# A selective-scan and attention kernel: state sums folded in pairs on POOL, B one step further ahead, and a new spacing of the work around the scan

## The chip, the cores and the metric

The kernel runs on one core of a Trainium2 chip. The metric is device time in microseconds of one execution. The kernel before takes 1438.1 us, the median of three runs (1437.43 to 1439.29). A core has a matmul engine (PE, with a weight-load port PEld), a vector engine (DVE), a scalar engine (ACT), a general engine (POOL) and a queue that issues transfers (SP). Each works through its own list of instructions in order, and waits on semaphores where it needs another's result. Matmuls write to eight banks of PSUM; everything else lives in SBUF.

## The reference

Input x is 4 images of 64x64 pixels with 96 channels. Two layers follow each other; layer normalisation and casts are left out here.

```python
# layer 0: group norm over 32 groups, layer norm, then a selective scan over the 4096 pixels
proj = xn @ W_in + b_in                      # value u, gate g, delta d, and A, B, C of 96 channels x 16 states
h = d * (A * h) + d * (B * u)                # a recurrence over the pixels, per channel and state
y = sigmoid(g) * sum_over_states(C * h)
x = x + (y @ W_out + b_out)
# layer 1: linear attention (no softmax), then an FFN with fp8 products and fp16 sums
t = t + attention(ln(t)) ; t = t + ffn(ln(t))
```

The scan is most of the work: 96 x 16 = 1536 recurrences over 4096 pixels for each of 4 images.

## The kernel before, in words

An image (a batch b) is cut into 8 chunks of 512 pixels, and a chunk into 12 tiles: 4 state groups (sh) of 4 states, times 3 channel groups (cg) of 32 channels. A tile is 128 recurrences (32 channels x 4 states on the partitions) over 512 pixels. There are 384 tiles, and one tile is one step of the main loop. For each tile:

- PE projects A, B and C (three matmuls each, line 175, a high and low split of float32) into the PSUM banks "A" (two), "B" (one) and "C" (one).
- ACT copies B with its bias to SBUF (b_copy, line 595, tile bu), and POOL multiplies it by du, the delta times the value (b_mul, line 598).
- DVE multiplies A by d in place in PSUM (a_mul, line 607), scans (line 614, tile h), and multiplies C by h (c_mul, line 632, tile ch). ACT keeps the scan's last column for the next chunk (keep, line 624).
- After every third tile PE sums the four states of a state group: three matmuls with the matrix fold, one for each channel group on its own 32 columns of the array (state_sum, line 645), added up over the four groups in the bank "Y". As the profile counts them, each is two instructions.

The order of work is written out by hand. The main loop (line 870) goes through steps s from FRONT = -22 on, and in each records: a_proj(s+1), c_proj(s), keep of the last tile, b_mul(s+1), scan(s), a_mul(s+1), c_mul(s); then whatever was registered for this step with at(step, fn), in the order of registration; then b_proj(s+2) and b_copy(s+2). ffn and tail are themselves called at their first step, and register their pieces then, so these stand last in a step. Nothing reorders the lists later. The pieces registered around the scan:

- front (line 496), for the chunk that comes about two later: the group norm is applied (POOL, lines 504 and 507), layer norm (stats on DVE, rstd on POOL, lines 327 and 328, apply on ACT, line 354), transposed, split into high and low (DVE lo, three transfers on SP), and projected to d, du and gate. d and du are each copied by 12 transfers on SP to tiles of 128 partitions (copies, line 531), tiles d4 and du4 with five buffers for three per chunk.
- tail (line 654): gating (yg), output projection, residual, layer norm, and the Gram matrix of the attention; attn_matrix (line 701) turns the latter into one 97x96 matrix per batch.
- ffn (line 740), for the batch before: attention, residual, layer norm, transpose, three hidden matmuls with relu and fp8 rounding (relu, quant), output projection, rounding and bias (y16, yb), store (o). It runs FFN0 = 15 steps into the next batch, one FFN per chunk; for the last batch it runs after the last tile (drain = True), an FFN every DRAIN_EVERY = 2 steps.
- group_norm (line 476), for the next batch: x is loaded, transposed by PE into the one bank "B" (gx_ps), and ACT takes sum and sum of squares from there (sums, line 412), eight times, from step GN0 = 22 of the batch on every GN_EVERY = 6 steps, loads 8 steps ahead; before them first() takes the mean of the first piece. Its last pieces give the scale and shift that front applies (diagonal builds the tile gdg, spread multiplies it out).

The small matmuls of front, tail, ffn and group norm share the two banks "M". Lengths in steps are given as places in a chunk of 12: "step 13" of a chunk is step 1 of the next.

Of the kernel before, what the change touches and what calls it, by code (L numbers as in the profile page):

```python
# [8 lines left out]
F32 = mybir.dt.float32  # L9
# [7 lines left out]
P = 128  # L17
# [20 lines left out]
FRONT = -22  # L38
GN0, GN_EVERY = 22, 6
FFN0 = 15  # L40
XBUFS = 2 * NCH + 5
DRAIN_EVERY = 2
# [3 lines left out]
def conv_attn_hybrid_kernel(  # L46
# [56 lines left out]
    nc.scalar.dma_start(bet, ln_beta.unsqueeze(1))  # L103
    raw0 = big.tile([C, A0], F32, tag="x", name="raw0", bufs=XBUFS)
    nc.scalar.dma_start(raw0, w_in[:, 0:A0])
    raws, brows = {}, {}
    for k, c0 in enumerate((B0, A0, C0)):
        for cg in range(NCG):
            t = big.tile([C, 32 * S], F32, tag="xat", name=f"raw{k}{cg}", bufs=NCH + 2)
            n0 = c0 + cg * 32 * S  # L110
            nc.scalar.dma_start(t, w_in[:, n0 : n0 + 32 * S])
            raws[k, cg] = t
        brows[k] = work.tile([NCG, 32 * S], F32, tag="ch", name=f"brow{k}", bufs=6)
        nc.scalar.dma_start(
            brows[k], b_in[c0 : c0 + C * S].rearrange("(g n) -> g n", g=NCG)
        )
# [108 lines left out]
    def bias(k):  # L225
        ps = bank("Y", [4, NSH * P], f"bias_ps{k}")
        for cg in range(NCG):
            for n, t in enumerate((betd[0], betd[0], betd[1])):
                nc.tensor.matmul(
                    ps, lhsT=t[:, cg, :], rhs=w_bac[k][:, n, cg],  # L230
                    start=(cg == 0 and n == 0), stop=(cg == NCG - 1 and n == 2),
                )
        row = work.tile([NCG, NSH * P], F32, tag="ch", name=f"bias{k}", bufs=6)
        nc.vector.tensor_tensor(
            row.rearrange("g (s c) -> g s c", s=S),
            ps[0:NCG].rearrange("g (s c) -> g s c", s=S),
            brows[k].rearrange("g (c s) -> g s c", s=S), ALU.add,
        )
        t_ps = bank("C", [P, NSH, NCG], f"biast_ps{k}")
        for sh in range(NSH):  # L240
            nc.tensor.transpose(
                t_ps[:, sh, :], row[:, sh * P : (sh + 1) * P], ident[:NCG, :NCG]
            )
        nc.vector.tensor_copy(b_bac[:, k], t_ps.rearrange("p h g -> p g h"))
# [17 lines left out]
    b2_q = const.tile([P, C], F32, name="b2_q")  # L262
    w1_sb = big.tile([P, NK, C], F32, tag="x", name="w1_sb", bufs=XBUFS)
    nc.scalar.dma_start(w1_sb, w1.rearrange("(m p) k -> p m k", p=P))
    w2_sb = big.tile([C, HID], F32, tag="x", name="w2_sb", bufs=XBUFS)
    nc.scalar.dma_start(w2_sb, w2)
    b1_sb = big.tile([NK, P], F32, tag="x", name="b1_sb", bufs=XBUFS)
    nc.scalar.dma_start(b1_sb, b1.rearrange("(m p) -> m p", p=P))
    b2_sb = big.tile([P, C], F32, tag="x", name="b2_sb", bufs=XBUFS)
    nc.scalar.dma_start(b2_sb, b2.partition_broadcast(P))  # L270
# [106 lines left out]
    class GroupNorm:  # L377
# [67 lines left out]
        def diagonal(self):  # L445
            self.dg = small.tile([C, 2, C], F32, tag="gdg", name=f"gdg_{self.b}", bufs=1)
            for k in range(2):
                nc.scalar.activation(
                    self.dg[:, k, :], ident[0:C, 0:C], AF.Copy, scale=self.m[:, k : k + 1]
                )  # L450
# [25 lines left out]
    def group_norm(b, s0):  # L476
        q = {}

        def make():
            q["g"] = GroupNorm(b)  # L480
            q["g"].first()

        def call(name, *args):
            getattr(q["g"], name)(*args)

        at(s0 + GN0 - 6, make)
        for n in range(NCH):
            at(s0 + GN0 + GN_EVERY * n - 8, load_x, b, n)
            at(s0 + GN0 + GN_EVERY * n, call, "sums", n)
        e = s0 + GN0 + GN_EVERY * (NCH - 1) + 1  # L490
        for n, name in enumerate(("moments", "mean", "root", "diagonal", "spread")):
            at(e + n, call, name)
# [79 lines left out]
    class Tile:  # L572
# [20 lines left out]
        def b_copy(self):  # L593
            self.bu = work.tile([P, TC], F32, tag="bu", name=f"bu_{self.nm}", bufs=4)
            nc.scalar.activation(self.bu, self.b_ps, AF.Identity, bias=self.bias(0))  # L595
# [16 lines left out]
        def scan(self):  # L612
            self.h = work.tile([P, TC], F32, tag="h", name=f"h_{self.nm}", bufs=3)
            nc.vector.tensor_tensor_scan(  # L614
                self.h, self.a_ps, self.bu,
                0.0 if self.i == 0 else state[self.sh, self.cg], ALU.mult, ALU.add,
            )
# [12 lines left out]
        def c_mul(self):  # L630
            self.ch = work.tile([P, TC], F32, tag="ch", name=f"ch_{self.nm}", bufs=6)
            nc.vector.scalar_tensor_tensor(  # L632
                self.ch, self.c_ps, self.bias(2), self.h, ALU.add, ALU.mult
            )

    tiles = {}
    y_ps = {}

    def state_sum(b, i, sh):

        g = b * NCH + i
        if sh == 0:
            y_ps[g] = bank("Y", [C, TC], f"y_ps_{b}_{i}")
        for cg in range(NCG):
            nc.tensor.matmul(  # L645
                y_ps[g][cg * 32 : (cg + 1) * 32, :], lhsT=fold,
                rhs=tiles.pop(g * NT + NCG * sh + cg).ch,
                start=(sh == 0), stop=(sh == NSH - 1),
                tile_position=(0, 32 * cg), skip_group_check=True,
            )  # L650
# [3 lines left out]
    def tail(b, i, s0):  # L654
# [39 lines left out]
        at(s0 + 6, lambda: ln.apply(xa, t))  # L694
        at(s0 + 7, gram)
        at(s0 + 8, keep)

# [3 lines left out]
    def attn_matrix(b, s0):  # L701
# [35 lines left out]
        for n, fn in enumerate((gram_out, gk, kv, ff, r)):  # L737
            at(s0 + 8 + n, fn)

    def ffn(b, i, s0, drain):  # L740
# [19 lines left out]
        def transpose():  # L760
            ps = bank("B" if drain else "M", [C, TC], f"xq_ps_{nm}")
            for j in range(J):
                nc.tensor.transpose(ps[:, j * P : (j + 1) * P], v["xn"][:, j, :], ident)
            v["xq"] = work.tile([C, TC], F8, tag="xq", name=f"xq_{nm}")
            nc.scalar.activation(v["xq"], ps, AF.Copy, saturate=False)

        def hidden(m):
            v["h", m] = bank(("C", "Y", "M")[m] if drain else "M", [P, TC], f"h_ps{m}_{nm}")
            nc.tensor.matmul(
# [3 lines left out]
        def relu(m):  # L773
            if m == 0:
                v["hq"] = work.tile([P, NK, TC], F8, tag="hq", name=f"hq_{nm}", bufs=1)
            h16 = work.tile([P, TC], F16, tag="h16", name=f"h16_{m}_{nm}")
            nc.scalar.copy(h16, v["h", m])  # L777
            hr = work.tile([P, TC], F16, tag="hr", name=f"hr_{m}_{nm}")
            bias = b1_q[:, m : m + 1]
# [9 lines left out]
        def project_out():  # L789
            ps = v["ps"] = bank("M", [P, J, C], f"y2_ps_{nm}")  # L790
            for j in range(J):
# [6 lines left out]
        def round_out():  # L798
            v["y16"] = work.tile([P, J, C], F16, tag="y16", name=f"y16_{nm}", bufs=1)
            nc.scalar.copy(v["y16"], v["ps"])  # L800

        def bias_out():
            v["yb"] = work.tile([P, J, C], F16, tag="yb", name=f"yb_{nm}", bufs=1)
            nc.gpsimd.tensor_tensor(  # L804
# [3 lines left out]
        def store():  # L808
            o = work.tile([P, J, C], F32, tag="o", name=f"o_{nm}", bufs=1)
            nc.gpsimd.tensor_tensor(o, t, v["yb"], ALU.add)  # L810
# [6 lines left out]
        at(s0 + 4, apply)  # L817
        at(s0 + 5, transpose)
        for m in range(NK):
            at(s0 + 6 + m, hidden, m)  # L820
            at(s0 + 7 + m, relu, m)
            at(s0 + 7 + m + drain, quant, m)
        at(s0 + 10 + drain, project_out)
        at(s0 + 11 + drain, round_out)
        at(s0 + 12 + drain, bias_out)
        at(s0 + 13 + drain, store)


# [15 lines left out]
    for b in range(B):  # L844
        for i in range(NCH):
            s0 = (b * NCH + i) * NT
            front(b, i, s0)
            for sh in range(NSH):
                at(s0 + NCG * (sh + 1), state_sum, b, i, sh)
            at(s0 + NT, tail, b, i, s0 + NT)  # L850
            if b < B - 1:
                at(s0 + NCH * NT + FFN0, ffn, b, i, s0 + NCH * NT + FFN0, False)
            else:
                e = K + FFN0 + DRAIN_EVERY * i
                at(e, ffn, b, i, e, True)
# [12 lines left out]

    s = FRONT
    while s < K or any(q >= s for q in steps):  # L870
        for k in (s, s + 1, s + 2):
            if 0 <= k < K and k not in tiles:
                tiles[k] = Tile(k)
# [4 lines left out]
        if 0 < s <= K:  # L878
            last.keep()
        if 0 <= s + 1 < K:  # L880
            tiles[s + 1].b_mul()
        if 0 <= s < K:
# [6 lines left out]
        call(s)  # L889
        if 0 <= s + 2 < K:  # L890
            tiles[s + 2].b_proj()
            tiles[s + 2].b_copy()
        s += 1
# [32 lines left out]
```

## Time and profile before

| What | Value |
|---|---|
| Median of three runs | 1438.1 us |
| The profiled execution | 1436.83 us |
| Its span, first to last instruction | 1435.1 us |
| Busy: PE, DVE, POOL, ACT | 1300.3, 1212.5, 747.2, 723.1 us |
| Granted PE clock, mean | 0.951 |
| First scan, last scan (start) | 71.1 us, 1347.5 us |
| State sums (line 645) | 768 instructions, 136.5 us busy |
| b_mul (line 598) | 384 instructions, 1286 ns each |

The profile is of one execution. "Busy" is the time in which an engine had an instruction in work; a matmul that is held up in the pipeline counts as busy. A line of the groups or of the timeline names the engine, the source line, the tiles (out<-in), the shape, and in brackets the idle time just before it and what ended it. The three parts of the span are the start (71 us: weights, first chunk's front), the loop, and what lies after the last tile (88 us).

### The profile page before, as it was taken

To read this page: it belongs to the slowest core of one execution; us is meant where nothing else is said; L and a number is where in the kernel's file an instruction comes from. 1 tells how busy PE (TensorE), PEld (TensorE's weight loads), DVE (VectorE), ACT (ScalarE), POOL (GpSimd) and SP (SyncE) were. 2 spreads that over 40 slices of the span, in tenths; PEclk is the share of its full clock that TensorE was granted. 3 is DMA by queue.
4 is the path that set the end of the run, shared out by engine and by line. 5 is a ranking of instruction groups with operands and counts; after the bars stand their busy time and mean duration, and the time that the engine had idled before them with its cause. 6 is when DMAs were issued, how large, how long until landed. Compare 5 with 4: busy or idle time off the path is not lost. (4 is left out here: it accounts for less than half of the span.)

```text
span 1435.1 us, 20740 instructions
## 1 busy us (share of the span) xinstructions
PE 1300.3 (91%) x6396; PEld 891.0 (62%) x6396; DVE 1212.5 (84%) x2309; ACT 723.1 (50%) x1658; POOL 747.2 (52%) x743
## 2 busy tenths in 40 slices
PE   2699988899999899899999998989999999999885
PEld 2356665666666666666666666666666666666562
DVE  2398988899998898899998888889999999999742
ACT  3234343433336555555555455665554555655555
POOL 3254544455554555555555555555556566545424
PEclk6699999999999999999999999999999999999955
DMA  6422222222222222222222122222222222222001
GB/s 156 107 61 56 49 55 61 48 54 54 54 59 51 69 51 56 57 47 60 60 50 70 45 62 57 58 52 58 59 49 49 51 60 59 50 49 51 12 6 44
DMA packets 81357, 80.98 MB, mean 56 GB/s; under 512 B 49617, under 2 KB 50101, under 8 KB 81246
## 3 DMA queue, kind: packets, MB, share of 16 engines
q1 hardware_dynamic: 78544, 77.22, 22.6%
q10 hardware_dynamic: 2702, 2.43, 0.7%
q8 instruction: 51, 0.84, 0.3%
q14 instruction: 60, 0.49, 0.1%
HBM read 8.72 MB, written 6.29 MB: 10 GB/s over the span
## 5 line engine op out<-in xcount | busy, mean ns | idle before, releaser
L598 POOL TENSOR_TENSOR bu<-bu,du 128x512 f32<-128x512 f32 x384 | 493.9, 1286 | 575.2 <-ACT bu L595 351.2
L614 DVE TENSOR_TENSOR_SCAN h<-Aps,state,bu 128x512 f32<-128x512 f32 x336 | 428.1, 1274 | 46.6 <-POOL bu L598 45.4
L595 ACT ACTIVATE bu<-Bps,b_bac 128x512 f32<-128x512 f32 x384 | 261.8, 682 | 398.2 <-PE Bps L175 386.2
L607 DVE SCALAR_TENSOR_TENSOR Aps<-Aps,b_bac,d 128x512 f32<-128x512 f32 x384 | 284.3, 740 | 64.5 <-PE Aps L175 63.8
L175 PE MATMUL Bps<-xs,w 128*128 128x512 f32 x768 | 271.0, 434 | 52.7 <-ACT gx_ps L412 37.6
L632 DVE SCALAR_TENSOR_TENSOR ch<-Cps,b_bac,h 128x512 f32<-128x512 f32 x384 | 285.5, 744 | 1.5 <-PE Cps L175 1.3
L175 PE MATMUL Cps<-xs,w 128*128 128x512 f32 x768 | 245.0, 401 | 3.0 <-DVE ch L632 2.9
L175 PE MATMUL Aps<-xs,w 128*128 128x512 f32 x768 | 241.7, 396 | 2.4 <-DVE h L614 2.1
L175 PEld LDWEIGHTS Bps<-xs,w 128*128 128x128 f32 x768 | 127.4, 191 | 102.1 <-ACT gx_ps L412 44.8
L175 PEld LDWEIGHTS Cps<-xs,w 128*128 128x128 f32 x768 | 142.1, 190 | 46.4 <-DVE ch L632 17.9
L175 PEld LDWEIGHTS Aps<-xs,w 128*128 128x128 f32 x768 | 145.4, 190 | 38.0 <-DVE h L614 4.1
L175 PE MATMUL Bps<-xl,w 128*128 128x512 f32 x384 | 152.6, 397 | 0.0
L175 PE MATMUL Aps<-xl,w 128*128 128x512 f32 x384 | 151.9, 395 | 0.0
L175 PE MATMUL Cps<-xl,w 128*128 128x512 f32 x384 | 151.6, 395 | 0.0
L645 PE MATMUL y_ps<-ch,fold 128*32 128x512 f32 x768 | 136.5, 605 | 0.0
L354 ACT ACTIVATE xa<-x,nmr_a,rstd_a 128x96 f32<-128x96 f32 x128 | 49.4, 457 | 105.0 <-DVE nmr_a L350 105.0
L354 ACT ACTIVATE z<-z,nmr_c,rstd_c 128x96 f32<-128x96 f32 x128 | 49.4, 457 | 78.1 <-DVE nmr_c L350 78.1
L175 PEld LDWEIGHTS Aps<-xl,w 128*128 128x128 f32 x384 | 72.8, 190 | 16.9
L175 PEld LDWEIGHTS Bps<-xl,w 128*128 128x128 f32 x384 | 72.6, 189 | 16.9
L175 PEld LDWEIGHTS Cps<-xl,w 128*128 128x128 f32 x384 | 72.8, 189 | 16.5
L787 ACT ACTIVATE hq<-hr 128x512 fp8e5<-128x512 f16 x96 | 60.6, 631 | 17.9 <-PE y_ps L793 8.2
L614 DVE TENSOR_TENSOR_SCAN h<-Aps,bu 128x512 f32<-128x512 f32 x48 | 58.1, 1211 | 11.0 <-POOL bu L598 10.9
(163 smaller groups left out, 1594.3 us busy)
## 6 DMA issues: line engine op xcount, KB each, us to landing
d<-d SPq DMA_DIRECT2D x384, 64.0 KB, 2.0
du<-du SPq DMA_DIRECT2D x384, 64.0 KB, 2.0
xl<-lo SPq DMA_DIRECT2D x64, 128.0 KB, 2.3
x<-in_x_dram SPq DMA_DIRECT2D x32, 192.0 KB, 2.8
out_dram<-o SPq DMA_DIRECT2D x32, 192.0 KB, 2.2
w<-w SPq DMA_DIRECT2D x6, 384.0 KB
xs<-lo SPq DMA_DIRECT2D x32, 64.0 KB, 2.0
raw<-in_L_conv_W_in_dram ACTq DMA_DIRECT2D x9, 192.0 KB, 4.5
```

Source lines behind the costliest of these rows:

```text
L175: nc.tensor.matmul(ps, lhsT=wt[:, n], rhs=mv, start=(n == 0), stop=(n == 2))
L354: nc.scalar.activation(dst[:, j, 0:C], src[:, j, :], AF.Identity, bias=nmr[:, j : j + 1], scale=self.r[:, j : j + 1],)
L595: nc.scalar.activation(self.bu, self.b_ps, AF.Identity, bias=self.bias(0))
L598: nc.gpsimd.tensor_tensor(self.bu, self.bu, rep["du4", self.b, self.i, self.cg], ALU.mult)
L607: nc.vector.scalar_tensor_tensor(self.a_ps, self.a_ps, self.bias(1), rep["d4", self.b, self.i, self.cg], ALU.add, ALU.mult,)
L614: nc.vector.tensor_tensor_scan(self.h, self.a_ps, self.bu, 0.0 if self.i == 0 else state[self.sh, self.cg], ALU.mult, ALU.add,)
L632: nc.vector.scalar_tensor_tensor(self.ch, self.c_ps, self.bias(2), self.h, ALU.add, ALU.mult)
L645: nc.tensor.matmul(y_ps[g][cg * 32 : (cg + 1) * 32, :], lhsT=fold, rhs=tiles.pop(g * NT + NCG * sh + cg).ch, start=(sh == 0), stop=(sh == ...
L787: nc.scalar.activation(v["hq"][:, m, :], v["hr", m], AF.Copy, saturate=False)
```

## The change

- After c_mul of an odd state group, POOL adds its ch tile to the ch tile of the even group before it (pair_sum); state_sum then runs for two groups at once, twice per chunk instead of four times.
- Tiles are made one step earlier: b_mul is recorded two steps ahead of its scan (was one), b_proj and b_copy three (were two). bu gets five buffers (four), ch eight (six), h two (three).
- tail starts one step later and its gram two; ffn starts at FFN0 = 26 and its pieces stand further apart; group norm at GN0 = 24, with its loads three steps ahead of its sums instead of eight.
- For the drain, FFN pieces use the banks C, B, Y, C and A instead of B, C, Y, M and M, and hq, y16, yb and o take the buffers of ch, d4, du4 and z. relu and quant of one piece now stand in the same step, and h16 and hr have one buffer instead of two.
- Some tiles move to other pools: raw0, w1_sb, w2_sb, b1_sb, b2_sb, and gdg, which shares a buffer with o. x has 22 buffers instead of 21.

```diff
-GN0, GN_EVERY = 22, 6
-FFN0 = 15
-XBUFS = 2 * NCH + 5
+GN0, GN_EVERY = 24, 6
+FFN0 = 26
+XBUFS = 2 * NCH + 6
...
-            self.dg = small.tile([C, 2, C], F32, tag="gdg", name=f"gdg_{self.b}", bufs=1)
+            self.dg = work.tile([C, 2, C], F32, tag="o", name=f"gdg_{self.b}", bufs=1)
...
-        at(s0 + GN0 - 6, make)
+        at(s0 + GN0 - 1, make)
         for n in range(NCH):
-            at(s0 + GN0 + GN_EVERY * n - 8, load_x, b, n)
+            at(s0 + GN0 + GN_EVERY * n - 3, load_x, b, n)
             at(s0 + GN0 + GN_EVERY * n, call, "sums", n)
...
-            self.bu = work.tile([P, TC], F32, tag="bu", name=f"bu_{self.nm}", bufs=4)
+            self.bu = work.tile([P, TC], F32, tag="bu", name=f"bu_{self.nm}", bufs=5)
...
-            self.h = work.tile([P, TC], F32, tag="h", name=f"h_{self.nm}", bufs=3)
+            self.h = work.tile([P, TC], F32, tag="h", name=f"h_{self.nm}", bufs=2)
...
+    def pair_sum(k):
+
+        t = tiles.pop(k).ch
+        s = tiles[k - NCG].ch
+        nc.gpsimd.tensor_tensor(s, s, t, ALU.add)
...
-                start=(sh == 0), stop=(sh == NSH - 1),
+                start=(sh == 0), stop=(sh == NSH - 2),
...
-        at(s0 + 7, gram)
-        at(s0 + 8, keep)
+        at(s0 + 8, gram)
+        at(s0 + 9, keep)
...
-            at(s0 + 8 + n, fn)
+            at(s0 + 10 + n, fn)
...
-                v["hq"] = work.tile([P, NK, TC], F8, tag="hq", name=f"hq_{nm}", bufs=1)
-            h16 = work.tile([P, TC], F16, tag="h16", name=f"h16_{m}_{nm}")
+                tag, bufs = ("ch", 8) if drain else ("hq", 1)
+                v["hq"] = work.tile([P, NK, TC], F8, tag=tag, name=f"hq_{nm}", bufs=bufs)
+            h16 = work.tile([P, TC], F16, tag="h16", name=f"h16_{m}_{nm}", bufs=1)
...
-            hr = work.tile([P, TC], F16, tag="hr", name=f"hr_{m}_{nm}")
+            hr = work.tile([P, TC], F16, tag="hr", name=f"hr_{m}_{nm}", bufs=1)
...
-        at(s0 + 5, transpose)
-        for m in range(NK):
-            at(s0 + 6 + m, hidden, m)
-            at(s0 + 7 + m, relu, m)
-            at(s0 + 7 + m + drain, quant, m)
-        at(s0 + 10 + drain, project_out)
-        at(s0 + 11 + drain, round_out)
-        at(s0 + 12 + drain, bias_out)
-        at(s0 + 13 + drain, store)
+        at(s0 + 6, transpose)
+        for m, d in enumerate((8, 9, 11)):
+            at(s0 + d, hidden, m)
+            at(s0 + d + 1, relu, m)
+            at(s0 + d + 1, quant, m)
+        at(s0 + (14 if drain else 17), project_out)
+        at(s0 + (15 if drain else 18), round_out)
+        at(s0 + (16 if drain else 19), bias_out)
+        at(s0 + (17 if drain else 20), store)
...
-            for sh in range(NSH):
-                at(s0 + NCG * (sh + 1), state_sum, b, i, sh)
-            at(s0 + NT, tail, b, i, s0 + NT)
+            for sh in range(0, NSH, 2):
+                for cg in range(NCG):
+                    at(s0 + NCG * (sh + 1) + cg + 1, pair_sum, s0 + NCG * (sh + 1) + cg)
+                at(s0 + NCG * (sh + 2) + 1, state_sum, b, i, sh)
+            at(s0 + NT, tail, b, i, s0 + NT + 1)
...
-                e = K + FFN0 + DRAIN_EVERY * i
+                e = K + 16 + DRAIN_EVERY * i
...
-        if 0 <= s + 1 < K:
-            tiles[s + 1].b_mul()
+        if 0 <= s + 2 < K:
+            tiles[s + 2].b_mul()
...
-        if 0 <= s + 2 < K:
-            tiles[s + 2].b_proj()
-            tiles[s + 2].b_copy()
+        if 0 <= s + 3 < K:
+            tiles[s + 3].b_proj()
+            tiles[s + 3].b_copy()
```

More of the change, by code (lines that the diff above doesn't have):

```diff
@@ L103, in conv_attn_hybrid_kernel @@
     nc.scalar.dma_start(bet, ln_beta.unsqueeze(1))
-    raw0 = big.tile([C, A0], F32, tag="x", name="raw0", bufs=XBUFS)
+    raw0 = big.tile([C, A0], F32, tag="xat", name="raw0", bufs=NCH + 2)
     nc.scalar.dma_start(raw0, w_in[:, 0:A0])
@@ L112, in conv_attn_hybrid_kernel @@
             raws[k, cg] = t
-        brows[k] = work.tile([NCG, 32 * S], F32, tag="ch", name=f"brow{k}", bufs=6)
+        brows[k] = work.tile([NCG, 32 * S], F32, tag="ch", name=f"brow{k}", bufs=8)
         nc.scalar.dma_start(
@@ L232, in bias @@
                 )
-        row = work.tile([NCG, NSH * P], F32, tag="ch", name=f"bias{k}", bufs=6)
+        row = work.tile([NCG, NSH * P], F32, tag="ch", name=f"bias{k}", bufs=8)
         nc.vector.tensor_tensor(
@@ L262, in conv_attn_hybrid_kernel @@
     b2_q = const.tile([P, C], F32, name="b2_q")
-    w1_sb = big.tile([P, NK, C], F32, tag="x", name="w1_sb", bufs=XBUFS)
+    w1_sb = work.tile([P, NK, C], F32, tag="ch", name="w1_sb", bufs=8)
     nc.scalar.dma_start(w1_sb, w1.rearrange("(m p) k -> p m k", p=P))
-    w2_sb = big.tile([C, HID], F32, tag="x", name="w2_sb", bufs=XBUFS)
+    w2_sb = work.tile([C, HID], F32, tag="ch", name="w2_sb", bufs=8)
     nc.scalar.dma_start(w2_sb, w2)
-    b1_sb = big.tile([NK, P], F32, tag="x", name="b1_sb", bufs=XBUFS)
+    b1_sb = work.tile([NK, P], F32, tag="h", name="b1_sb", bufs=2)
     nc.scalar.dma_start(b1_sb, b1.rearrange("(m p) -> m p", p=P))
-    b2_sb = big.tile([P, C], F32, tag="x", name="b2_sb", bufs=XBUFS)
+    b2_sb = work.tile([P, C], F32, tag="h", name="b2_sb", bufs=2)
     nc.scalar.dma_start(b2_sb, b2.partition_broadcast(P))
@@ L630, in c_mul @@
         def c_mul(self):
-            self.ch = work.tile([P, TC], F32, tag="ch", name=f"ch_{self.nm}", bufs=6)
+            self.ch = work.tile([P, TC], F32, tag="ch", name=f"ch_{self.nm}", bufs=8)
             nc.vector.scalar_tensor_tensor(
@@ L760, in transpose @@
         def transpose():
-            ps = bank("B" if drain else "M", [C, TC], f"xq_ps_{nm}")
+            ps = bank("C" if drain else "M", [C, TC], f"xq_ps_{nm}")
             for j in range(J):
                 nc.tensor.transpose(ps[:, j * P : (j + 1) * P], v["xn"][:, j, :], ident)
-            v["xq"] = work.tile([C, TC], F8, tag="xq", name=f"xq_{nm}")
+            tag, bufs = ("bu", 5) if drain else ("xq", 1)
+            v["xq"] = work.tile([C, TC], F8, tag=tag, name=f"xq_{nm}", bufs=bufs)
             nc.scalar.activation(v["xq"], ps, AF.Copy, saturate=False)
         def hidden(m):
-            v["h", m] = bank(("C", "Y", "M")[m] if drain else "M", [P, TC], f"h_ps{m}_{nm}")
+            v["h", m] = bank("BYC"[m] if drain else "M", [P, TC], f"h_ps{m}_{nm}")
             nc.tensor.matmul(
@@ L789, in project_out @@
         def project_out():
-            ps = v["ps"] = bank("M", [P, J, C], f"y2_ps_{nm}")
+            ps = v["ps"] = bank("A" if drain else "M", [P, J, C], f"y2_ps_{nm}")
             for j in range(J):
@@ L798, in round_out @@
         def round_out():
-            v["y16"] = work.tile([P, J, C], F16, tag="y16", name=f"y16_{nm}", bufs=1)
+            tag, bufs = ("d4", 5) if drain else ("y16", 1)
+            v["y16"] = work.tile([P, J, C], F16, tag=tag, name=f"y16_{nm}", bufs=bufs)
             nc.scalar.copy(v["y16"], v["ps"])
         def bias_out():
-            v["yb"] = work.tile([P, J, C], F16, tag="yb", name=f"yb_{nm}", bufs=1)
+            tag, bufs = ("du4", 5) if drain else ("yb", 1)
+            v["yb"] = work.tile([P, J, C], F16, tag=tag, name=f"yb_{nm}", bufs=bufs)
             nc.gpsimd.tensor_tensor(
@@ L808, in store @@
         def store():
-            o = work.tile([P, J, C], F32, tag="o", name=f"o_{nm}", bufs=1)
+            if drain:
+                o = big.tile([P, J, C], F32, tag="z", name=f"o_{nm}")
+            else:
+                o = work.tile([P, J, C], F32, tag="o", name=f"o_{nm}", bufs=1)
             nc.gpsimd.tensor_tensor(o, t, v["yb"], ALU.add)
@@ L869, in conv_attn_hybrid_kernel @@
     s = FRONT
+    made = set()
     while s < K or any(q >= s for q in steps):
-        for k in (s, s + 1, s + 2):
-            if 0 <= k < K and k not in tiles:
+        for k in (s, s + 1, s + 2, s + 3):
+            if 0 <= k < K and k not in made:
+                made.add(k)
                 tiles[k] = Tile(k)
```

## The prediction

> **What bounds the kernel now.** I read the page first, then the windows, then the waits and the timeline of one chunk. Two windows (columns: us from the start; length; busy time of PE, weight load, DVE, ACT, POOL; granted clock; DMA):
>
> ```profile
> 480.00:520.00 40.00, 36.16 (x191) 25.06 (x190) 35.12 (x65) 23.45 (x56) 21.36 (x21) 1.00 0.26 63
> 1200.00:1240.00 40.00, 39.44 (x198) 26.84 (x196) 37.16 (x70) 22.74 (x54) 23.06 (x23) 1.00 0.22 53
> ```
>
> The loop has two regimes. Where the next batch's group norm runs (480), PE idles a tenth; elsewhere (1200) PE shows full and DVE is close behind. Lengths of chunks of 12 steps come from the starts of the scans (timeline):
>
> ```profile
> 309.40 1.27 DVE L614 TENSOR_TENSOR_SCAN h<-Aps,state,bu 128x512 f32<-128x512 f32 x1
> 345.48 1.28 DVE L614 TENSOR_TENSOR_SCAN h<-Aps,state,bu 128x512 f32<-128x512 f32 x1
> 544.48 1.28 DVE L614 TENSOR_TENSOR_SCAN h<-Aps,state,bu 128x512 f32<-128x512 f32 x1 [0.68 <-POOL bu L598]
> 587.00 1.28 DVE L614 TENSOR_TENSOR_SCAN h<-Aps,state,bu 128x512 f32<-128x512 f32 x1 [0.68 <-POOL bu L598]
> 1196.52 1.28 DVE L614 TENSOR_TENSOR_SCAN h<-Aps,state,bu 128x512 f32<-128x512 f32 x1
> 1235.64 1.28 DVE L614 TENSOR_TENSOR_SCAN h<-Aps,state,bu 128x512 f32<-128x512 f32 x1
> ```
>
> So 36.1 us with neither FFN nor group norm, 42.5 with both, 39.1 with FFN alone; with group norm alone the scans give 39.9 to 41.6.
>
> "PE full" is partly back-pressure. From start to next start, a projection takes 0.70 us, a state sum 0.99; 36 projections, four sums and the small matmuls (dug 3x0.70, o_ps 0.82, a_ps 0.92, xat and gram 1.03, y2 0.51, the rest 1.5) make 36 of the 39.1. DVE's own floor: 2.50 us from scan to scan without other work, 12 times, and 6.0 of other work (stats 3x0.93, lo 0.66, du 0.65, yg 0.59, residuals 0.90, the rest 0.4): 36.0. The 3 us between are waits like these:
>
> ```profile
> 1226.86 1.28 DVE L614 TENSOR_TENSOR_SCAN h<-Aps,state,bu 128x512 f32<-128x512 f32 x1 [0.96 <-POOL bu L598]
> 1233.09 1.28 DVE L614 TENSOR_TENSOR_SCAN h<-Aps,state,bu 128x512 f32<-128x512 f32 x1 [0.96 <-POOL bu L598]
> 1210.36 0.76 DVE L607 SCALAR_TENSOR_TENSOR Aps<-Aps,b_bac,d 128x512 f32<-128x512 f32 x1 [0.49 <-PE Aps L175]
> ```
>
> Twice per chunk the scan waits for bu: ACT copies it late, behind a layer norm. In group norm PE also waits for the one B bank, where ACT takes its sums:
>
> ```profile
> 561.69 0.72 PE L175 MATMUL Bps<-xs,w 128*128 128x512 f32 x2 [1.64 <-ACT gx_ps L412]
> ```
>
> A third queue matters, SP's. The third d copy of a chunk overwrites what a_mul of tile 9 reads, so it and the 12 du copies behind it wait for that a_mul (waits of SP's own queue, and the timeline, where tile 9's a_mul ended at 1225.25):
>
> ```profile
> SPq L531 <- DVE Aps L607: 176.3, 31, 8.1
> 1225.28 2.41 SPq L531 DMA_DIRECT2D d<-d  x4
> 1227.73 7.55 SPq L531 DMA_DIRECT2D du<-du  x12
> ```
>
> **What the Trainium skill says.** "SBUF — State Buffer", "SBUF: two separate sides": VectorE and GpSimd lock each other out only where VectorE's operation has two SBUF inputs or a two-port mode. Scan, a_mul and c_mul each have one input in PSUM; the trace agrees: c_mul takes 0.745 us wholly under POOL work and 0.741 without. I charge POOL's new work nothing on DVE. "GPSIMD Engine Reference", "Elementwise — side-by-side cycle accounting": about 2.6 cycles per element for two inputs; 512 at 1.2 GHz are 1.1 us plus dispatch (an estimate); b_mul measures 1.286 and, back to back, 1.25, which I use for the add. "DMA: Bandwidth & Descriptors", "Anatomy of one DMA": a semaphore wait happens on the issuing sequencer; the SP lines above show it: everything behind waits too.
>
> **The change part by part.** Steps are counted from a chunk's first tile, so tile 12 is the next chunk's first.
>
> *Half the state sums go.* Two sums of 0.99 us per chunk, 64 in all: 63 us of PE work. PE's floor falls to 34, below DVE's 36.0; alone this is worth at most the distance to DVE.
>
> *B a step ahead.* b_copy and b_mul have one step (2.5 us) more before their scan: the two waits of 0.96 go. Their cover is the extra bu buffer. h with two buffers makes scan(s+2) wait for ACT's keep(s), behind b_copy(s+3). At step 7, where ACT waits for nmr, keep ends 2.31 us after the next scan's start and is needed at 2.50 (by 1219.69 to 1222.0): 0 us, with 0.2 to spare.
>
> *192 adds on POOL*, 1.25 us each: 7.5 per chunk, to 31 of 39. What matters is where they stand. At steps 4 to 6 POOL is clear by the time PE wants the sum (step 7): 0. At steps 10 to 13 its queue reads b_mul(12), add(9), o, b_mul(13), add(10), b_mul(14), add(11), and PE's sum at step 13 waits for add(11), with b_proj(16) and a_proj(15) behind it, and DVE's a_mul(15) behind these. b_mul(12) is now a step earlier and meets the du copies: the first tile's last one landed at 1231.71, 6.46 us after tile 9's a_mul ended. This makes a cycle, a_mul(9) to a_mul(21): a_mul 0.73; du landed 6.46 and 0.05; POOL 6x1.25 + 0.92 = 8.4, and 0.15 for semaphores; the last column group's two passes about 0.85 (between 0.33, a third of the sum, and 1.05, as after the loop), hidden 0.24, b_proj 0.70, a_proj with its latency 0.90; then DVE's six steps 15.0 and their other work 5.2. Sum 38.7, against 39.1 before. Without FFN (no o 0.92, no hidden 0.24, DVE 1.47 less): 36.1, as before. So the gain in PE work is almost wholly returned at step 13.
>
> *Group norm moved.* Its sums fall on steps 6 and 12 instead of 4 and 10. At 6, PE has slack (three short projections) and ACT does them ahead of the layer norm: about 0. At 12, x is loaded three steps ahead instead of eight, behind the du copies: 10.03 us from tile 9's a_mul to the end of their issue, 2.75 until x lands. Cycle: 0.73 + 10.03 + 2.8 + gx 0.4 + ACT and latencies 1.7 + b_proj 0.70 + a_proj 0.90, then seven DVE steps 17.5, their other work 5.85 and 0.3 = 40.9 with FFN, 39.4 without. The wait at step 13 is inside it. first() at step 23 meets the same x: from it and the next sum 3.9 more per batch (5.7 and 2.1, less what overlaps).
>
> Chunks 1 to 5 of a batch with group norm, before from the scans: 203.9, 211.8, 214.0. After: 36.1 + 4x39.4 + 3.9 = 197.6; 36.1 + 4x40.9 + 3.9 = 203.6 (FFN starts 11 steps later, so chunk 1 has none); 38.7 + 4x40.9 + 3.9 = 206.2. Together -22.3. The eleven other FFN chunks: -0.4 each, -4.4.
>
> *Buffers.* gdg now shares o's buffer: twice POOL's o stands behind the matmul that spreads gdg, a step late: 2.5 each, +5. M banks stay one use per step: 0. x's 22nd buffer: 0.
>
> *After the loop.* The last add 1.3; FFN's layer norm now ahead of the tail's in ACT's queue 2.4; against it no y2 in front of the first attention (3.0) but one attention more (1.0): +1.7. In the drain before, hq had one buffer:
>
> ```profile
> 1394.84 0.63 ACT L787 ACTIVATE hq<-hr 128x512 fp8e5<-128x512 f16 x1 [2.44 <-PE y_ps L793]
> ```
>
> Periods were 6.9 and later 5.6 us per FFN. After, hq is free but h16 and hr have one buffer each: ACT does three times copy, wait for DVE, quantise (1.52 from start to start at 1407.93), and 1.0: 5.5. Eight of these save some 5, and one non-drain FFN more lies there (8.4 us of ACT, partly in the fill): 0, between -8 and +8.
>
> *Small waits* that the two cycles leave out (a_mul(16) and (17) get their bank with 0.1 to 0.2 to spare): 0.2 x 27 chunks = +5.
>
> Sum: -22.3 - 4.4 + 5 + 1.7 + 0 + 5 = -15. The profiled execution took 1436.8 us (span 1435.1), 1.3 below the median 1438.1: 1436.8 - 15 + 1.3 = 1423, say 1424.
>
> **Rivals.**
> *The adds arrive in time* (0.2). If POOL gets through earlier than I reckon, chunks without group norm fall to DVE's floor, 36.6 with its small waits; 14 chunks gain some 2 more, chunk 1 too: 1393. For it: POOL is idle a fifth of the time; against: the du landing.
> *The cycle through POOL and SP is longer* (0.3), the slower side. Place: the sum at step 13. Each 0.1 us costs 2.7 us over 27 chunks; from 0.55 us more the gain is gone. For it: du copies for tile 14 land 11.5 us after a_mul(9) and POOL wants them at 12.4, so one us of delay in SP or POOL goes through. At 1.2 us more: 1456.
> *Nothing in sum* (0.1): the cycle 0.55 longer, 1438.
> Mine: 0.4, own range 1408 to 1433.
>
> **How the numbers follow.** A measurement of this kernel tells 0.2% (2.9 us) from no change. Faster is mine and the first rival, 0.6; same 0.1; slower 0.3. The range leaves out the tails of the two outer cases: 1390 to 1454.
>
> **What would show it.** State sums 384 instead of 768 instructions, 68 us of busy time. POOL near 990 us. Scans waiting for bu: gone but for the first tiles of a chunk. PE's state sum waiting 2 to 3 us for POOL's ch every 12 steps, at the second sum only; gx_ps waiting for DMA x at every second sum. Chunks of 38.7 and 41. I am wrong if the sum at step 13 doesn't wait (then 1393), or if it waits over 3.5 us.

## The result and the profile after

The changed kernel takes 1460.0 us (median of 4 runs, 1457.75 to 1460.16), the kernel before 1438.4 (1437.43 to 1439.29): a ratio of 1.0147, 95% interval 1.0129 to 1.0164. The change makes it slower. The prediction was 1424, range 1390 to 1454; the sign was wrong and the range too low.

The profiled execution took 1457.75 us, its span is 1456.0, 20.9 longer than before. First the same two windows (columns: us from the start; length; busy time of PE, weight load, DVE, ACT, POOL; granted clock; DMA):

```profile
480.00:520.00 40.00, 34.19 (x158) 24.04 (x157) 34.36 (x65) 21.58 (x53) 26.16 (x24) 0.96 0.21 50
1200.00:1240.00 40.00, 36.92 (x183) 26.44 (x182) 37.40 (x72) 21.91 (x52) 30.53 (x29) 1.00 0.23 54
```

At 1200, where FFN runs alone, PE is 2.5 us less busy than before, as half the state sums are gone, and POOL 7.5 more; DVE is as busy as it was. At 480, beside the group norm, PE and DVE are both less busy, PE in part because of the halved sums. The starts of the scans give the chunks (timeline of DVE; the first three lines bound two chunks with FFN and group norm, the last two one chunk with FFN alone):

```profile
551.66 1.28 DVE L614 TENSOR_TENSOR_SCAN h<-Aps,state,bu 128x512 f32<-128x512 f32 x1
...
596.14 1.27 DVE L614 TENSOR_TENSOR_SCAN h<-Aps,state,bu 128x512 f32<-128x512 f32 x1
...
642.41 1.27 DVE L614 TENSOR_TENSOR_SCAN h<-Aps,state,bu 128x512 f32<-128x512 f32 x1
...
1173.49 1.27 DVE L614 TENSOR_TENSOR_SCAN h<-Aps,state,bu 128x512 f32<-128x512 f32 x1
...
1212.22 1.27 DVE L614 TENSOR_TENSOR_SCAN h<-Aps,state,bu 128x512 f32<-128x512 f32 x1
```

With both, 44.5 and 46.3 us against 42.5 before; with FFN alone 38.7, and its neighbours 39.7 to 40.0, against 39.1. Added up over the span, from the same starts:

| part of the span | before, us | after, us | difference | predicted |
|---|---|---|---|---|
| up to the first scan | 71.1 | 70.7 | -0.4 | - |
| chunk 0 of batch 0 | 34.4 | 32.0 | -2.4 | - |
| chunks 1 to 5 of batches 0, 1, 2 (group norm) | 629.7 | 646.1 | +16.4 | -22.3 |
| chunks 6, 7 of batch 0 and 0 of batch 1 | 108.3 | 110.7 | +2.4 | 0 |
| the twelve full chunks with FFN alone | 469.4 | 469.7 | +0.3 | -4.4 |
| last chunk to its last scan | 34.7 | 35.2 | +0.5 | - |
| after the last scan | 87.6 | 91.6 | +4.0 | +1.7 |

The prediction's +5 of small waits, 0.2 us in each of 27 chunks, stands outside this column: 3 of it belong to the fifteen chunks with group norm, 2.4 to the twelve with FFN alone. So does its +5 for the buffer of gdg.

The loss is for the most part in the group norm, and there the waits name it (waits of all engines: us in total, times, longest):

```profile
DVE Aps L607 <- PE Aps L175: 120.7, 95, 7.1
...
PE gx_ps L387 <- DMA x<-in_x_dram: 38.8, 18, 4.3
...
PEld y_ps L651 <- POOL ch L643: 28.4, 23, 2.5
...
POOL bu L598 <- DMA du<-du: 22.2, 12, 3.7
```

PE waits 38.8 us for x; before, 5.7. After the first scan it is 29.4 us in twelve waits, and none before. DVE's waits for A's projection rise from 63.8 to 120.7 us. One such place step by step (timeline, the passage from chunk 4 to chunk 5 of batch 1, the longest of the nine of its kind; the a_mul of tile 9 ended at 586.76):

```profile
586.79 2.41 SPq L531 DMA_DIRECT2D d<-d  x4
...
589.24 8.34 SPq L531 DMA_DIRECT2D du<-du  x12
...
597.63 0.58 SPq L93 DMA_DIRECT2D x<-in_x_dram  x1
...
600.79 1.06 PE L387 MATMUL gx_ps<-ident,x 128*96 128x128 f32 x4 [2.61 <-DMA x<-in_x_dram]
...
603.49 1.22 PE L175 MATMUL Bps<-xs,w 128*128 128x512 f32 x2 [1.64 <-ACT gx_ps L412]
...
606.45 0.76 DVE L607 SCALAR_TENSOR_TENSOR Aps<-Aps,b_bac,d 128x512 f32<-128x512 f32 x1 [6.55 <-PE Aps L175]
```

The order is that of the prediction: third d copy, twelve du copies, then x, gx, ACT's sums, B, A, a_mul. But B's first passes take 1.22 us where they took 0.73 at 593.09, and A's 1.05 instead of 0.62. The granted clock (the last column but two) is half there, as windows around it show:

```profile
593.00:600.60 7.60, 5.08 (x23) 3.80 (x23) 6.70 (x8) 3.87 (x10) 7.28 (x7) 1.00 0.50 121
600.60:607.40 6.80, 4.97 (x13) 3.45 (x13) 0.76 (x1) 4.52 (x10) 2.37 (x2) 0.50 0.01 2
607.50:614.30 6.80, 6.80 (x39) 5.09 (x38) 6.50 (x9) 3.37 (x7) 3.05 (x3) 1.00 0.33 77
```

At the end of PE's wait for x the clock goes to half and stays there 6.8 us, so the chain behind x runs slower. Between first and last scan the trace shows eleven such stretches, 58 us in all, ten of them in group norm chunks; before there were four of 3.4 us. The Trainium skill, "TensorE: Matmul & The Clock Gate", Part 1, says that this clock is at half after an idle window of about 3.4 us and full again after a busy one. The trace agrees in the size of the stretches, 3.41 and 6.83 us. It does not agree that the window must be idle: the wait was 2.61 us, and in the 3.41 us before the clock fell PE was busy for 0.98. The last section comes back to this.

The wait at step 13 is there too (timeline, a chunk with FFN alone):

```profile
1255.93 1.05 PE L651 MATMUL y_ps<-ch,fold 128*32 128x512 f32 x4
1256.01 1.26 POOL L643 TENSOR_TENSOR ch<-ch,ch 128x512 f32<-128x512 f32 x1
...
1257.33 1.05 PE L651 MATMUL y_ps<-ch,fold 128*32 128x512 f32 x2 [0.35 <-POOL ch L643]
...
1260.12 0.76 DVE L607 SCALAR_TENSOR_TENSOR Aps<-Aps,b_bac,d 128x512 f32<-128x512 f32 x1 [1.32 <-PE Aps L175]
```

PE does two thirds of the sum, stands for add(11), and then spends a full 1.05 us on the last column group. a_mul(15) waits 1.32 us for what is queued behind.

### The profile page after: what moved, and what is told of

The parts are those of the page before. It is cut to its first block, busy times and chain, and to the rows that moved or that the text cites. A ratio compares the mean times of both kernels' runs of the same rounds, so it can differ in the third digit from the quotient of the medians.

```text
span 1456.0 us, 20065 instructions
## 1 busy us (share of the span) xinstructions
PE 1247.2 (86%) x6012; PEld 894.7 (61%) x6012; DVE 1229.5 (84%) x2309; ACT 724.2 (50%) x1658; POOL 982.7 (67%) x935
## 4 chain that ended last, share of the span: by engine, by line
PE 42%; DVE 16%; ACT 10%; SPq 9%; issue 8%; DMA 8%; POOL 7%; ACTq 0%; POOLq 0%; DVEq 0%
PE Bps L175 11%; PE Cps L175 9%; PE Aps L175 9%; SPq L531 9%; DVE h L614 4%; DVE ch L632 4%; POOL bu L598 3%; PE y_ps L651 3%; DMA du<-du 2%; ACT gx_ps L412 2%; DMA x<-in_x_dram 2%; PE dug_ps L175 2%; ACT xa L354 2%; DMA d<-d 2%; ACT z L354 2%
## 5 line engine op out<-in xcount | busy, mean ns | idle before, releaser
L607 DVE SCALAR_TENSOR_TENSOR Aps<-Aps,b_bac,d 128x512 f32<-128x512 f32 x384 | 283.9, 739 | 123.1 <-PE Aps L175 120.7
L175 PE MATMUL Bps<-xs,w 128*128 128x512 f32 x768 | 276.0, 441 | 88.0 <-ACT bu L595 46.6
L175 PE MATMUL Cps<-xs,w 128*128 128x512 f32 x768 | 249.0, 406 | 7.2 <-DVE ch L632 6.5
L643 POOL TENSOR_TENSOR ch<-ch,ch 128x512 f32<-128x512 f32 x192 | 247.1, 1287 | 0.5 <-DVE ch L632 0.5
L651 PE MATMUL y_ps<-ch,fold 128*32 128x512 f32 x384 | 88.7, 619 | 11.6 <-POOL ch L643 11.6
L354 ACT ACTIVATE xn<-x,nmr_f,rstd_f 128x96 f32<-128x96 f32 x96 | 37.0, 456 | 65.9 <-DVE nmr_f L350 65.9
```

The lines of the kernel that those rows point to most:

```text
L175: nc.tensor.matmul(ps, lhsT=wt[:, n], rhs=mv, start=(n == 0), stop=(n == 2))
L354: nc.scalar.activation(dst[:, j, 0:C], src[:, j, :], AF.Identity, bias=nmr[:, j : j + 1], scale=self.r[:, j : j + 1],)
L607: nc.vector.scalar_tensor_tensor(self.a_ps, self.a_ps, self.bias(1), rep["d4", self.b, self.i, self.cg], ALU.add, ALU.mult,)
L643: nc.gpsimd.tensor_tensor(s, s, t, ALU.add)
L651: nc.tensor.matmul(y_ps[g][cg * 32 : (cg + 1) * 32, :], lhsT=fold, rhs=tiles.pop(g * NT + NCG * sh + cg).ch, start=(sh == 0), stop=(sh == ...
```

## The experiments

Theory X: the loss is the late load of x. It is loaded three steps ahead, and SP reaches it only behind the third d copy and the du copies, which wait for the a_mul of tile 9. Theory B, the rival, lays the loss on other parts of the change, so that moving the loads does little. A further question was what each part is worth once X is out of the way: the adds, B's step, the group norm's steps.

| run | edit | median, us | ratio to before, 95% |
|---|---|---|---|
| after | the change | 1460.0 | 1.0147 (1.0129-1.0164) |
| e1 | after, loads eight steps ahead | 1404.5 | 0.9747 (0.9724-0.9770) |
| e2 | before, seven of eight loads three ahead | 1515.6 | 1.0521 (1.0497-1.0545) |
| e3 | after without adds, four sums | 1453.4 | 1.0090 (1.0072-1.0108) |
| e7 | after, du copies ahead of the third d copy | 1399.4 | 0.9712 (0.9697-0.9728) |
| e8 | e7, second sum at step 14 | 1385.6 | 0.9630 (0.9606-0.9655) |
| e9 | e7 without adds, four sums | 1404.9 | 0.9765 (0.9740-0.9790) |
| e10 | before, du copies ahead of the third d copy | 1442.3 | 1.0019 (1.0007-1.0031) |
| e11 | e7, B at its old steps | 1411.5 | 0.9811 (0.9786-0.9836) |
| e12 | e7, group norm at its old steps | 1435.7 | 0.9971 (0.9963-0.9980) |
| e14 | after, first load of a batch eight ahead | 1437.1 | 0.9979 (0.9967-0.9990) |

The median of before was 1438.4, 1440.8, 1438.6 and 1439.6 in the four sets, so times of different sets are comparable to some 2 us.

**e1, loads early in the changed kernel.**

```diff
-            at(s0 + GN0 + GN_EVERY * n - 3, load_x, b, n)
+            at(s0 + GN0 + GN_EVERY * n - 8, load_x, b, n)
```

> The changed kernel with x loaded eight steps ahead of its group norm sums again, instead of three; nothing else differs. Theory X (the loss is the late x: the load stands in SP's queue behind the du copies, PE waits at the sum of step 12 and at first(), and its clock falls during the wait): the nine late sums lose some 4 us of their delay each and the three firsts some 5, so 1410 to 1420 us, GN chunks with FFN near 40.5. Theory B (the loss is the one B bank and ACT's sums, wherever x is): little changes, 1450 or more.

55 us less, more than X had asked for. PE no longer waits for x after the first scan; what is left lies in the start (waits):

```profile
DVE Aps L607 <- PE Aps L175: 74.8, 95, 5.2
...
PE gx_ps L387 <- DMA x<-in_x_dram: 8.4, 6, 3.9
```

Group norm chunks fall from 646.1 to 594.1 us in all, and only one half-clock stretch of 3.4 us is left between the scans. B falls.

**e2, loads late in the kernel before.** It does the reverse, in the kernel that has none of the rest of the change:

```diff
-            at(s0 + GN0 + GN_EVERY * n - 8, load_x, b, n)
+            at(s0 + GN0 + GN_EVERY * n - (3 if n else 8), load_x, b, n)
```

> The kernel before, with the suspected cost alone added: x for the sums 1 to 7 is loaded three steps ahead instead of eight. In this kernel the sums 2, 4 and 6 fall on step 10, and their loads on step 7, behind the d and du copies. Theory X: nine sums wait 5 to 8 us each, so 1480 to 1510 us. Theory B: below 1450.

75 us more than before, somewhat over X's range. The wait for x is the one that grew (waits; it was 5.7 in before):

```profile
PE gx_ps L387 <- DMA x<-in_x_dram: 70.7, 10, 8.0
```

A chunk whose last scan interval holds such a wait takes 49.7 to 51.6 us instead of 39.9 to 43.3. The late load is enough by itself.

**e7, the queue's order instead of the distance.** x stays three steps ahead, but the d copy that made SP wait goes behind du; copies gets the channel groups as an argument:

```diff
-            copies("d4", v["d"])
+            copies("d4", v["d"], (0, 1))
...
             copies("du4", du)
+            copies("d4", v["d"], (2,))
```

> The changed kernel with the twelve du copies put ahead of the third d copy in SP's queue, so that du no longer waits for tile 9's a_mul, and x waits behind four copies instead of sixteen. Theory X: as with early loads, 1405 to 1420 us. If du's late landing also sets the cycle through POOL, chunks without group norm fall from 39.1 by up to 0.5; if ACT's copy of B sets it, they stay.

61 us less, below X's range. PE's waits for x fall to 9.9 us, all before the first scan. SP's queue in the timeline shows what moved (the end of chunk 4 of batch 1, whose scan 12 starts at 564.4):

```profile
543.10 4.97 SPq L531 DMA_DIRECT2D d<-d  x8
549.07 7.47 SPq L531 DMA_DIRECT2D du<-du  x12
556.64 2.43 SPq L531 DMA_DIRECT2D d<-d  x4
559.12 0.58 SPq L93 DMA_DIRECT2D x<-in_x_dram  x1
```

du no longer stands behind the d copy that needs tile 9's buffer. x still follows that copy, but it is issued 5.3 us before scan 12, where in the lines of after it was issued 1.5 us behind it. Against e1 it has one thing more: du is early as well. POOL's waits for du, 22.2 us after and 29.0 in e1, are one of 4.6 here, and the twelve chunks with FFN alone take 38.8 us on average, where after has 39.1.

**e10, the same order in the kernel before.**

> The kernel before with the du copies ahead of the third d copy, nothing else. Theory X: in the kernel before nothing on the path stands behind these copies (x is loaded before them, b_mul is held by ACT), so the order on SP is worth nothing there: 1432 to 1441. Rival: the order gains by itself, and the 39 us it gave in the changed kernel have nothing to do with where x is loaded: 1400 to 1420.

No gain (0.07 to 0.31% slower; the median is 1.3 us above X's range). So the order gains nothing by itself: the 61 us belong to what the change put behind those copies.

**e14, only first()'s x early.**

```diff
-            at(s0 + GN0 + GN_EVERY * n - 3, load_x, b, n)
+            at(s0 + GN0 + GN_EVERY * n - (3 if n else 8), load_x, b, n)
```

> The changed kernel (1460.0 us), with only the first of a batch's eight x loads eight steps ahead, the other seven three ahead as they are. Theory X, with x late at each load: first() loses about 7 us in each of three batches, and going back to an early first x brings that: 1436 to 1443, with the chunks behind unchanged at 43 to 46. As the prediction had it (3.9 a batch) it brings 12: 1446 to 1450. Rival: the wait moves to the next load instead: over 1455.

23 us less, inside X's range; the wait doesn't move to the next load. Chunk 2 of each batch takes 39.9, 40.8 and 41.3 instead of 46.8, 48.1 and 48.3; the chunks behind stay at 40 to 46. So the late first x costs 7 us per batch. That isn't the same quantity as the prediction's 3.9, as the expectation above took it: this x serves first() and the sum after it, and the 3.9 came on top of a chunk that already had a late x at its sum.

**e3 and e9, without the adds**: four state sums at the steps of their groups, no adds on POOL, first in the changed kernel and then in e7. The last sum, now that of sh = 3, closes the accumulation.

```diff
-            for sh in range(0, NSH, 2):
-                for cg in range(NCG):
-                    at(s0 + NCG * (sh + 1) + cg + 1, pair_sum, s0 + NCG * (sh + 1) + cg)
-                at(s0 + NCG * (sh + 2) + 1, state_sum, b, i, sh)
+            for sh in range(NSH):
+                at(s0 + NCG * (sh + 1) + 1, state_sum, b, i, sh)
```

> The changed kernel without POOL's adds: the four state sums per chunk are PE's again, each one step after its last tile; B stays a step ahead, the rest too. If the adds give nothing in sum because PE waits for the last of them at step 13 (my prediction's cycle): PE does two sums more but waits for none, chunks without group norm 37.5 to 38.5 instead of 39.1, about 1440 us. If the adds pay (PE's work bounds the chunk): 39.5 or more per chunk, 1470.

> The kernel with the du copies ahead of the third d copy (1399.4 us), but with four state sums a chunk and no adds. In the run of after without adds, FFN chunks took 37.7 (with adds 38.7 here), and the scan interval in which a chunk with group norm does its first sums 4.66 instead of 3.76. Theory W: adds lose 1.0 in each of 14 FFN chunks and gain about 1.2 in each of 15 group norm chunks: 1396 to 1404, no difference. Rival: the adds are the gain of the change: 1415 or more; or only a loss: 1388 or less.

In the changed kernel the adds lose 7 to 8 us; with x in time they gain 6 to 8. e3's chunks, 37.7, were as its first case had them, its total, 1453.4, lies between the two forecasts. Theory W's 1396 to 1404 for e9 was close: 1404.9. The chunks show two opposite effects. A chunk with FFN alone takes 37.7 without adds, less than with them: the wait at step 13 costs more than the two sums that are saved. Over twelve such chunks the adds lose 14.0 us in the changed kernel and 9.2 in e7, where du is early. In the fifteen group norm chunks they gain, 12.7 us in the changed kernel and 17.0 in e7. So what the adds are worth depends on the other parts, and in the changed kernel it comes out negative.

**e8, the second sum a step later** (with e7's order):

```diff
-                at(s0 + NCG * (sh + 2) + 1, state_sum, b, i, sh)
+                at(s0 + NCG * (sh + 2) + (2 if sh else 1), state_sum, b, i, sh)
```

> The kernel with the du copies ahead of the third d copy (1399.4 us), and in it the second state sum of a chunk at step 14 instead of 13. Theory W: the wait for add(11) at step 13 is what brings back most of the gain in PE work; a step later the add has landed, the third scan interval falls from 4.55 to about 3.15 us in 14 FFN chunks and from 3.56 to 3.1 in the others without group norm: 1.3 x 14 + 0.4 x 6 = 21 less: 1375 to 1383. Rival V: DVE and PE are at their floors there, or the tail's gating becomes the wait: 1395 or more.

1385.6 us, 12 to 14 less than e7; W had said 16 to 24, so the place is right and the gain somewhat smaller. The sum no longer waits for POOL (timeline, FFN alone):

```profile
1151.69 1.30 POOL L644 TENSOR_TENSOR ch<-ch,ch 128x512 f32<-128x512 f32 x1
...
1153.90 1.06 PE L652 MATMUL y_ps<-ch,fold 128*32 128x512 f32 x6
```

All six passes run together in 1.06 us, 0.9 after the add. Such chunks take 37.4 us, and state sums 69.3 us in the whole kernel where after has 88.7. Against e9, measured beside it, the adds with this later step are worth 19.4 us. This is the fastest kernel of the study, 3.7% below before.

**e11, B back at its old steps** (with e7's order):

```diff
-        if 0 <= s + 2 < K:
-            tiles[s + 2].b_mul()
+        if 0 <= s + 1 < K:
+            tiles[s + 1].b_mul()
...
-        if 0 <= s + 3 < K:
-            tiles[s + 3].b_proj()
-            tiles[s + 3].b_copy()
+        if 0 <= s + 2 < K:
+            tiles[s + 2].b_proj()
+            tiles[s + 2].b_copy()
```

> The kernel with the du copies ahead of the third d copy (1399.4 us), with B's projection, copy and multiply back at their old steps. Theory W: the step further ahead is what pays: the two waits of 0.96 per chunk come back, less what the wait at step 13 hides: 15 to 45 more, 1415 to 1445. Rival: the state sums on PE pay and B ahead is nothing: 1396 to 1403.

12 to 14 us more, just under the range that W gave and above the rival's. The two waits come back as before (timeline):

```profile
1158.40 1.28 DVE L615 TENSOR_TENSOR_SCAN h<-Aps,state,bu 128x512 f32<-128x512 f32 x1 [0.95 <-POOL bu L599]
...
1164.62 1.28 DVE L615 TENSOR_TENSOR_SCAN h<-Aps,state,bu 128x512 f32<-128x512 f32 x1 [0.95 <-POOL bu L599]
```

But a chunk with FFN alone grows only from 38.7 to 38.9, because the interval of the sum at step 13 falls from 4.55 to 3.1 us: the two waits stand for each other. Most of the loss is in the group norm chunks, 601.2 us in all against 592.7. Where no wait at step 13 is in the way, B's step may be worth more; that was not run.

**e12, group norm back at its old steps** (with e7's order): GN0 = 22, first() six steps ahead, loads eight ahead.

> The kernel with the du copies ahead of the third d copy (1399.4 us), with the group norm's steps as in the kernel before: sums at steps 4 and 10, first() six steps ahead of them, x loaded eight ahead. The prediction took the sums at their new steps for nothing once x is there. In the chip's runs with x in time, a chunk with them still takes 1.2 us (FFN) to 2.2 us (no FFN) more than one without; in the kernel before 3.4 to 5. Theory G: the new steps are worth the difference, some 2.4 in each of 15 chunks, and going back costs it: 1415 to 1435. Rival: the shares of B's bank and ACT's two sums cost the same at any step: 1396 to 1404.

36 us more, just over theory G's range; the rival falls. PE has no wait for x after the first scan. Chunks 1 to 5 take 207.9, 211.5 and 214.3 us, where e7 has 192.3, 199.0 and 201.4, and the kernel before 203.9, 211.8 and 214.0. In this setting no gain in group norm chunks is left without the new steps: at the old ones they cost what they did before, even with the B step and half the sums. It is not theirs alone, as at the new steps the adds (17.0) and B's step (8.5) have a share too. The trace shows fourteen half-clock stretches between the scans, 51 us, though no x is late; e7 has two. Which of the shared bank, ACT's sums and the moved FFN pieces opens the idle time behind them was not taken apart.

## Why the prediction was wrong

**What failed: "Group norm moved".** Chunks 1 to 5 were to take 607.4 us; they took 646.1. That is 38.7 too low, where the whole forecast was 36 too low; the other steps nearly cancel. The mechanism was the predicted one, x behind the du copies; the length of the cycle was mis-sized:

- *The cycle from a_mul(9) to a_mul(14)* was 17.3 us in the prediction's sum (0.73 + 10.03 + 2.8 + 0.4 + 1.7 + 0.70 + 0.90). Over the nine passages with one late x it takes 17.7 to 20.5, 18.9 on average: 1.6 more. The end of the DMA issue came 10.25 after the a_mul (+0.2); x was there 3.1 later, not 2.8 (+0.3); gx and ACT's sums took 2.3, not 2.1 (+0.2); B and A took 2.5, not 1.6 (+0.9). In the lines above, the longest case, it is 606.45 - 586.00 = 20.45, and B and A take 2.96.
- *From a_mul(14) to a_mul(21)* it had 23.15 on average (seven DVE steps and their other work); these take 24.3, 1.2 more.
- The half clock, of which the prediction had nothing, goes with most of this. In the two of the nine passages without such a stretch the cycle to a_mul(14) is 17.7 and 17.9, B and A take 1.69, and the chunk comes out 0.8 and 1.0 over its forecast. In the seven others it comes out 2.5 to 4.7 over.
- *first()* had 3.9 per batch on top of a late sum, and this was nearly right: the three chunks that hold it are 10.2 over the forecast together, 3.4 each, where the nine others are 3.0 over each (26.7 in all).
- Chunk 1 of the three batches is 1.9 over.

With x in time the same chunks take 594.1 us (e1), less than the 607.4 forecast. So the rest of the change gains 36 us there, and the late x takes 52 back; the prediction had -22 for the two together. It gave the gain of the new steps no term of its own ("At 6 ... about 0"), and e12 shows that without them there is none.

**A term put at nothing.** "I charge POOL's new work nothing on DVE", because scan, a_mul and c_mul each have an input in PSUM. c_mul did stay at 742 ns. But nmr_c, a small product in front's layer norm, has both inputs in SBUF, which is the case that its own rule excepts (timeline, the first line before, the others after):

```profile
1229.36 0.17 DVE L350 SCALAR_TENSOR_TENSOR nmr_c<-mv_c,rstd_c 128x4 f32<-128x4 f32 x1
...
1245.32 1.29 POOL L598 TENSOR_TENSOR bu<-bu,du 128x512 f32<-128x512 f32 x1
1245.68 0.95 DVE L350 SCALAR_TENSOR_TENSOR nmr_c<-mv_c,rstd_c 128x4 f32<-128x4 f32 x1
```

It ends 0.02 us after b_mul. In after 25 of the 32 nmr_c do so and take 0.96 us; in all 25.2 us against 5.4 before. So it is in every run with B a step ahead (23 to 27 of 32, without the adds too), and in none with B at its old steps (before, e2, e10, e11). B's step moved b_mul onto nmr_c. In a chunk with FFN alone the three scan intervals around the two waits of 0.96 take 8.7 us after and 9.8 before: nearly half of the gain is lost between them, 0.8 of it in nmr_c. What this costs in the whole was not run.

**What held.**
- "Half the state sums go ... the gain in PE work is almost wholly returned at step 13": chunks with FFN alone were forecast at 38.7 before small waits and took 39.1 on average, as before. The wait is shorter than the 2 to 3 us foretold: 1.25 us of the weight load and 0.35 of PE in the lines above, 40.0 us in 36 waits in all. e8 takes it away and gets 37.4. The last column group's passes, taken at 0.85 between 0.33 and 1.05, measured 1.05. State sums took 88.7 us and not 68, as each second one is done in two goes.
- "B a step ahead: the two waits of 0.96 go": idle time before the scan fell from 46.6 to 0.4 us. Its two-buffer h shows no cost: no scan waits for keep.
- 192 adds at 1.25: they measured 1.287 each, 247 us; POOL is busy 982.7 us (forecast near 990).
- b_mul(12) meets the du copies: POOL waits for du twelve times, 22.2 us. In e7 this is one wait, and the FFN chunks are 0.35 us shorter.
- Small waits: with their 2.4 the chunks with FFN alone were forecast at -2.0 and measured +0.3. (The prediction counted eleven of the twelve.)
- After the loop: the last y is gated 4.6 us after the last scan instead of 3.3, which is the last add's 1.3; rmat is there 2.1 later after the last scan than before, against 1.7 forecast. The drain gave another 1.9, inside the -8 to +8. The +5 for the buffer that gdg shares with o shows in no interval that I could name.

**The rivals.** The slower rival's 1456 comes near the result by luck, for its place does not: the cycle at step 13 cost no more than forecast. The slower side was to be found in the part that the prediction had booked as its largest gain. Its working said that x comes behind the du copies, and priced that from durations at full clock. It had no rival in which this one term was a few us larger, though 1 us of it, taken at twelve chunks, is 12 us of the result.

## What to carry to other kernels

A DMA issue that waits for a buffer holds everything behind it on its queue, so before moving a load closer to its use read what that queue waits for at that step; a load that needs nothing belongs in front of a copy that must wait. A path priced at full clock can take longer where PE is left half idle: look at the granted clock of the stretch. A saving on the busiest engine is worth little while the partial sums are asked for before they exist: with x in time, one step of slack raised the worth of these adds from 6 to 8 us to 19. A small instruction can lose more than a large one when work moves on another engine: look at its duration too.

## What the runs showed that was not expected

- The clock follows PE's busy share, and short waits are enough to lose it. Between the first and the last scan of the twelve traces it fell to half 76 times. Within a run all changes lie on one grid of 3.413 us. In the 3.413 us before a fall PE was busy for at most 0.50 of the time, in 32 of the 76 without a single idle piece over 1.7 us. Of 4273 such windows after which the clock stayed full, the lowest share was 0.44, and eight were under 0.50. It came back after a window with a share of 0.88 or more, and stayed half after shares up to 0.82. Around the place shown above (windows of after, same columns):

```profile
597.19:600.60 3.41, 0.98 (x7) 0.59 (x5) 2.71 (x4) 0.23 (x2) 3.41 (x4) 1.00 0.62 153
600.60:604.01 3.41, 1.58 (x5) 1.14 (x6) 0.00 (x0) 2.00 (x6) 1.09 (x1) 0.50 0.01 3
604.01:607.43 3.42, 3.42 (x9) 2.31 (x7) 0.76 (x1) 2.52 (x5) 1.28 (x1) 0.50 0.00 0
```

  PE is busy for 0.29 of the first window, and the clock halves; for 0.46 of the second, and it stays; for all of the third, and it is full from there on. Busy time is the profile's, with modelled ends, and no run varied this share alone. It fits that after, with its waits for x, has eleven such stretches in the loop, e1 and e7 one and two, and e12, with other idle time, fourteen.
- Twelve du copies took 7.5 to 7.6 us to issue in most chunks of before, after and e7, about 0.63 each, and 7.7 to 9.1 in the others. Why is open.
